# A two-layer decoder on one core: the end of layer 1's cross attention, the routing of its last four tiles, and the shared expert's place, re-ordered

## The chip, the cores and the metric

The kernel runs on one core of a Trainium2 chip. Its time is in device microseconds (us), as the median of several runs; lower is better. PE is the TensorE matmul engine (PEld its weight load), DVE is VectorE, ACT is ScalarE, POOL is GpSimd and SP is SyncE, which issues most transfers. A "send" below is one indirect DMA that POOL issues.

## The reference, cut to what matters

3200 tokens (32 batches of 100) of width 256 go through two decoder layers; each has self attention, cross attention to 361 context rows and a mixture of experts, each on a normalized copy of x and added to x. The change touches the last two blocks of layer 1:

```python
# cross attention: 16 heads of 64, softmax over 361 context rows
attn = softmax(q @ k.T * scale);  x = x + (attn @ v) @ Wo + bo
# experts: 64 in 8 groups, the best 4 groups, then the best 8 experts; 256 places an expert
scores = sigmoid(xn @ gate.T);  topk_idx, topk_w = ...      # routing
out    = sum over a token's experts of  w * w2(silu(xe w1) * (xe w3))
shared = silu(xn @ sg.T) * (xn @ su.T) @ sd.T                # every token
x = x + out + shared
```

## The kernel before, in words

Tokens lie in 25 tiles of 128 rows (`f`), batches are 100 rows (`b`), so a tile is complete when its last batch is.

**Cross attention (`l1_xattn`, L702).** The order of PE is written out by hand. Each batch has 13 steps `s` (L837 on): `scores` (L748; a matmul of 361 columns, DVE's maximum, ACT's exp, DVE's scaling), and three steps later `turn` (L761; three PE transposes, evacuated by ACT to `eT`). At step 3 of batch b the whole of batch b-1 is multiplied with its values (`values`, L769: 48 instructions, evacuated by DVE to `zT`). `between` (L802) puts further work into the steps: the next batch's values (`vals1`), queries (`queries`, `absorbed`, in alternate batches), and `out` (L785), the output projection of a finished tile in two parts, after which DVE adds it to `x` and takes the norm's statistics. `out` stands at steps 1 and 2 of the batch two after the tile's last one; in the last batch also at steps 11 and 12.

**Routing (`route`, L1516).** When the last tile of a group in `ROUTED` (L47: seven groups of three, then two groups of two) is out, a generator is appended to `self.routes`. Each `tick` (L1677) advances each generator by one piece: DVE normalizes the rows, PE turns them and multiplies them with the gate, ACT takes a sigmoid, DVE finds groups and experts, PE counts places (`pp`: operands `tmp`,`before` and `acc`,`ones`), DVE computes `slot`, and then one send per tick: 8 sends a tile (`x_d<-xr,slot`, L1628), each held by `depend` until the last recorded work of its tick. There is one tick a step up to batch 28 and two a step from batch 29 on (L858). The last group (tiles 23 and 24) is advanced by hand in `last_tile` (L820) and in `l1_ffn` (L1698). `list1` (L1639) then makes `listi`, the list of experts in use. `norm_stats` has ACT's Sqrt, the gate ACT's Sigmoid, the softmax ACT's Exp, the experts ACT's Silu: each change between them is one ACT_TABLE_LOAD.

**Shared expert (`shared1`, L1754).** A generator: `hidden(f, i)` is half of the hidden columns of four tiles (8 matmuls of 512 columns on PE, Silu on ACT, a product on DVE), `down(f)` is one tile's second projection (4 matmuls of 256 columns) and DVE's addition to `x`. Before, two `hidden` lie behind the last turns of the cross attention, four `down` around the last tile's norm, then 5 `hidden` and 9 `down` in `l1_ffn` until `FIRST1` = 25 (L59) is used up, and the rest beside the experts' units, about 1 us a unit.

**Units (`units`, L1795).** 24 whole units (256 rows) and 8 half ones. For each, SP issues the expert's weights (`we`, 384 KB, after reading `listi`), and its rows (`xe<-x_d`, up to 321 KB, 8 buffers); the rows wait for `flag` (L1726), which POOL sets when all sends have landed. PE turns the rows (`expert_turn`), multiplies (`expert_hidden`, `expert_add`), DVE weights the result, and POOL adds it to memory by an indirect DMA for each 128 rows (`sum<-ye,xe`, L1897), each behind the landing of the unit two before it. SP issues nine units' weights first, then five units' rows, then a pair a unit. At the end `flag_u` (L1846) releases the loading of the sums, the last additions and the output.

Of the kernel before, what the change touches and what calls it, by code (L numbers as in the profile page):

```python
# [9 lines left out]
F32 = mybir.dt.float32  # L10
# [6 lines left out]
P = 128  # L17
NB = 32
# [25 lines left out]

HALVES = {0: 6, 6: 6, 12: 6, 18: 7}
EDGES = {0: 6, 6: 6, 12: 6, 18: 3, 21: 2, 23: 2}
ROUTED = {**{f: 3 for f in range(0, 21, 3)}, 21: 2, 23: 2}  # L47
FRONT0 = {**{f: 4 for f in range(0, 20, 4)}, 20: 5}
FRONT1 = {0: 4, **{f: 3 for f in range(4, NF, 3)}}
RG = 3  # L50
# [5 lines left out]
WHOLE, HALF = 24, 8  # L56
UNITS = WHOLE + HALF

FIRST1 = 25.0  # L59

BLOCKS0 = 29

# [6 lines left out]
def tile_of(b):  # L69

    f = tiles_before(b + 1)
    return f - 1 if f > tiles_before(b) else None
# [12 lines left out]
class Kernel:  # L85
# [597 lines left out]
    def turn_wk1(self):  # L683

        wk = self.w1x[1]
        for c in range(0, 8, 4):
# [2 lines left out]
                self.nc.tensor.transpose(pt[:, j, :], wk[:, c + j, :], self.ident)  # L689
            self.evac(wk[:, c : c + 4, :], pt, self.ahead_of)  # L690

    def vals1(self, b, half, c):

        if c == 0:
            self.v1[b, half] = self.kv.tile([KC, NKC, 512], F32, tag="v", name="v", bufs=AHEAD)
        t = self.v1[b, half, c] = self.v1[b, half]
        pm = self.bank_p()[:KC, :]
        wv = self.w1x[2]
        self.mm(pm, [(self.ctx1[b][:, c * KC : (c + 1) * KC], wv[:, half * 512 : (half + 1) * 512])])
        return self.evac(t[:, c, :], pm, self.ahead_of)  # L700

    def l1_xattn(self):  # L702
        nc, tc, a = self.nc, self.tc, self.a
        self.route_begin()
        with ExitStack() as st:
# [14 lines left out]
            self.routes = []  # L720
            self.z_begin(pool, 8)
            self.ahead_of = 1

            def queries(b0, u):

# [59 lines left out]
            def out(f, part):  # L785
# [10 lines left out]
                for f0, n in ROUTED.items():  # L796
                    if f0 + n == f + 1 < NF:
                        self.routes.append([self.route(f0, n), None])

            VALS = {4: (0, 0), 5: (0, 1), 6: (0, 2), 7: (1, 0), 9: (1, 1), 10: (1, 2)}  # L800

            def between(b, s):  # L802

                if s in VALS and b + 1 < NB and (b + 1, *VALS[s]) not in self.v1:
                    self.vals1(b + 1, *VALS[s])
                if b % 2 == 0 and b + 2 < NB and s in (8, 11, 12):
                    queries(b + 2, (8, 11, 12).index(s))
                if b % 2 and b + 1 < NB and s == 0:
                    queries(b + 1, 3)
                f = tile_of(b - 2) if b > 1 else None  # L810
                if s in (1, 2) and f is not None:
                    out(f, s - 1)
                if b == NB - 1 and s > 10:
                    out(tile_of(b - 1), s - 11)
                if s == 11 and 0 < b < 5:
                    f = 16 + 2 * b
                    n = min(2, NF - f)
                    self.norm_turn(f, n, self.norm_rows(f, n, bias=self.xbo1), self.bank_p())

            def last_tile():  # L820
                f, shared = NF - 1, self.shared
                for part in range(2):
                    out(f, part)
                    if part == 0:
                        next(shared)
                        next(shared)
                while self.routes:
                    self.tick(self.after)
                r = self.last_route = self.route(NF - 2, 2)
                next(r)  # L830
                next(shared)
                next(shared)

                for _ in range(10):
                    next(r)

            with tc.manual_schedule(engines={mybir.EngineType.PE}):  # L837
                for u in range(4):
                    queries(0, u)
                for p in range(2):  # L840
                    absorbed(0, p, 2)
                for b in range(NB):
                    if b + 2 < NB and b + 2 not in self.ctx1:
                        self.load1(b + 2)
                    for s in range(NS):
                        n = NS * b + s
                        if s < 4:
                            scores(n)
                        if 2 < s < NS - 1:
                            scores(n + 1)  # L850
                        if s == 3 and b > 0:
                            values(b - 1)
                        if s in (3, 8) and b % 2 and b + 1 < NB:
                            absorbed(b + 1, s // 8)
                        between(b, s)
                        if n > 2:
                            turn(n - 3)
                        for _ in range(1 + (b > NB - 4)):  # L858
                            self.tick(self.after)
                n = NS * NB  # L860
                self.shared = self.shared1(first)
                turn(n - 3)
                next(self.shared)
                turn(n - 2)
                turn(n - 1)
                next(self.shared)
                values(NB - 1)
                last_tile()


# [645 lines left out]
    def route(self, f, G):  # L1516
# [7 lines left out]
        if G == RG:  # L1524
            xr = rp.tile([P, RG, XROW], F32, tag="xr", name="xr", bufs=2)
        else:
            xr = self.lnp.tile([P, 2, XROW], F32, tag="xn", name="xr2")
        nc.gpsimd.tensor_copy(xr.bitcast(I32)[:, :, D], self.tok[:, f : f + G])
        for j in range(G):
            self.norm_row(f + j, xr[:, j, :D], nc.vector)  # L1530
# [223 lines left out]
    def shared1(self, first):  # L1754

        nc, x = self.nc, self.x
        wg, wu, wd = self.w1s
        hT = {0: first[:, : 8 * P].rearrange("p (i n) -> p i n", i=2)}

        def hidden(f, i):  # L1760

            n = min(4, NF - f) * P
            if f and i == 0:
                o = f // 4 % 2 * 8 * P
                hT[f] = self.wbs[:, o : o + 8 * P].rearrange("p (i n) -> p i n", i=2)
            pg, pu = self.bank_s()[:, :n], self.bank_t()[:, :n]
            for p, ws in ((pg, wg), (pu, wu)):
                self.mm(p, [(ws[:, k, i * P : (i + 1) * P], self.xn_at(k, f, n // P)) for k in range(NK)])
            g = self.wbs[:, (16 + 4 * i) * P : (20 + 4 * i) * P] if f else first[:, 8 * P : 12 * P]
            nc.scalar.activation(g[:, :n], pg, AF.Silu)  # L1770
            nc.vector.tensor_tensor(hT[f][:, i, :n], pu, g[:, :n], ALU.mult)
            return 3.5

        def down(f):
            pd = self.bank_m()[:, :D]
            h, at = hT[f // 4 * 4], slice(f % 4 * P, (f % 4 + 1) * P)
            self.mm(pd, [(h[:, i, at], wd[:, i, :]) for i in range(2)])
            nc.vector.tensor_tensor(x[:, f, :], pd, x[:, f, :], ALU.add)
            return 0.9

        for i in range(2):
            yield hidden(0, i)
        for f in range(4):
            yield down(f)
        for f in range(4, NF + 4, 4):
            for i in range(2):
                if f < NF:
                    yield hidden(f, i)
                for j in range(2):
                    if f > 4 and f - 4 + 2 * i + j < NF:  # L1790
                        yield down(f - 4 + 2 * i + j)


# [1 line left out]
    def units(self, pool, units, beside=None):  # L1795
# [5 lines left out]
        def weights(i):  # L1801
            we[i] = pool.tile([P, 768], F32, tag="we", name="we", bufs=12)
            u = units[i][0]
            e = nc.sync.value_load(self.listi[0:1, E1 + u : E1 + u + 1], min_val=0, max_val=E1 - 1)
            nc.sync.dma_start(we[i], self.a["wexp"][bass.ds(e, 1)].rearrange("o p n -> p (o n)"))
# [13 lines left out]

        with tc.manual_schedule(engines={mybir.EngineType.PE}):  # L1820
            room = 0.0
            for i in range(9):
                weights(i)
            for i in range(5):
                rows(i)
            for i in range(n_all + 2):
                if i + 5 < n_all:
                    rows(i + 5)
                if i + 9 < n_all:
                    weights(i + 9)  # L1830
                if i < n_all:
                    self.expert_turn(pool, i, len(units[i][1]), xes, xTs)
                if 0 <= i - 1 < n_all:
                    self.expert_hidden(pool, i - 1, len(units[i - 1][1]), we[i - 1], xTs, hTs)

                if beside and i > 2:
                    room = room + 1.0 if i < n_all else 100.0
                    while room > 0:
                        took = next(beside, None)
                        if took is None:  # L1840
                            break
                        room -= took
                if 0 <= i - 2:
                    self.expert_add(pool, i - 2, units[i - 2], we.pop(i - 2), xes, hTs, added, beside)
        flag = pool.tile([1, 1], F32, tag="flag", name="flag_u", bufs=2)
        flag = nc.gpsimd.memset(flag, 0.0)  # L1846
        self.depend(flag, added[0] + added[1], "the units' sums")
# [175 lines left out]
```

## Time and profile before

| what | value |
|---|---|
| median of 3 runs | 3042.85 us (3042.25 to 3046.59) |
| the profiled execution | 3043.06 us, of which the span is 3041.3 us |
| mean granted TensorE clock | 0.978 |
| PE busy | 2905.4 us, 96% of the span |
| DVE, ACT, POOL busy | 1786.2, 1410.3, 910.8 us |
| first turn of a unit's rows | 2877.73 us from the span's start |
| `flag_u` set | 3008.23 us |

Read it so: a line of a timeline has the start, the time taken, the engine, the line, the operation, its tiles (out<-in), the shape and the count of merged instructions, and in brackets how long the engine had sat idle before and what ended that ("issue": nothing that the profile shows). The windows have each engine's busy time in a stretch, the granted clock (1.00 is full), the share of the 16 DMA engines and GB/s. PE carries out each fp32 matmul of the program as two entries, so 48 instructions of `values` are `x96`.

### The profile page before, as it was taken

How to read it: one execution, taken by the hardware profiler on the slowest of the kernel's cores; microseconds unless marked ns; L12 is line 12 of the kernel's file. 1: busy time of each engine (PE TensorE's matmuls, PEld its weight loads, DVE VectorE, ACT ScalarE, POOL GpSimd, SP SyncE). 2: the span in 40 equal slices, each digit the busy share in tenths (PEclk: the TensorE clock that was granted, in tenths of full speed). 3: DMA queues.
4: the chain of work that ended last, by engine and by line, in shares of the span. 5: the costliest groups of instructions: out<-in, count | busy, mean ns of one | idle time of the engine just before them, and what ended most of it. 6: DMA issues, size and time to landing. Idle time of an engine off the chain costs nothing.

```text
span 3041.3 us, 66443 instructions
## 1 busy us (share of the span) xinstructions
PE 2905.4 (96%) x26074; PEld 2210.0 (73%) x26074; DVE 1786.2 (59%) x5048; ACT 1410.3 (46%) x4257; POOL 910.8 (30%) x1038
## 2 busy tenths in 40 slices
PE   8999999999999999999998999999999999998893
PEld 6777777677777757888885667777777777775582
DVE  6666656577777732222225778676676766765353
ACT  5554555566666621222223224556566565665120
POOL 3221222366656543000005530011311302132364
PEclk9999999999999999999999999999999999998997
DMA  8860000000000032555562100000000000000386
GB/s 315 287 242 1 1 1 1 14 17 16 15 15 15 5 116 98 192 188 186 184 232 89 38 2 10 9 30 29 25 14 9 14 9 13 10 12 4 101 207 189
DMA packets 127924, 224.75 MB, mean 74 GB/s; under 512 B 39373, under 2 KB 106245, under 8 KB 120816
## 3 DMA queue, kind: packets, MB, share of 16 engines
q1 hardware_dynamic: 97680, 126.30, 13.0%
q0 software_dynamic: 26640, 90.80, 9.0%
q8 instruction: 210, 3.44, 0.5%
q10 hardware_dynamic: 3280, 3.28, 0.3%
q14 instruction: 114, 0.93, 0.1%
HBM read 152.75 MB, written 112.56 MB: 87 GB/s over the span
## 4 chain that ended last, share of the span: by engine, by line
PE 57%; DVE 3%; DMA 2%; issue 2%; ACT 0%; another core or an unknown queue 0%; POOL 0%; POOLq 0%; SPq 0%; DVEq 0%; ACTq 0%
PE ps_t L141 35%; PE ps_t L778 5%; PE ps_t L766 5%; PE ps_t L1328 4%; PE ps_t L790 3%; PE ps_s L141 2%; DMA sum<-ye,xe 1%; PE ps_m L141 1%; PE ps_t L993 1%; PE ps_t L1334 1%; DMA wA<-sum 1%; DVE s L983 1%; PE ps_t L216 1%; PE ps_t L1272 0%; DVE x_sb L1241 0%
## 5 line engine op out<-in xcount | busy, mean ns | idle before, releaser
L1628 POOL DMA_INDIRECT x_d<-xr,slot x200 | 195.2, 976 | 686.9 <-DVE m L754 396.7
L141 PE MATMUL ps_t<-xnT,wA 128*128 128x200 f32 (+1 forms) x1600 | 326.8, 348 | 1.8 <-DMA wA<-in_wq 1.2
L141 PE MATMUL ps_t<-cT,q 128*128 128x361 f32 x832 | 321.1, 475 | 1.5 <-DVE q L136 1.5
L757 ACT ACTIVATE wBx<-ps_t,m 128x361 f32<-128x361 f32 x416 | 235.0, 566 | 163.2 <-DVE m L754 156.0
L141 PEld LDWEIGHTS ps_t<-xnT,wA 128*128 128x128 f32 x1600 | 270.3, 191 | 31.9 <-issue 14.6
L767 ACT COPY eT<-ps_t 124x384 f32<-124x384 f32 (+1 forms) x416 | 193.3, 474 | 207.9 <-PE ps_t L766 176.7
L141 PE MATMUL ps_t<-xT,w 128*128 128x256 f32 x1276 | 283.2, 381 | 0.7 <-ACT xT L135 0.7
L141 PEld LDWEIGHTS ps_t<-xT,w 128*128 128x128 f32 x1276 | 240.0, 190 | 41.7 <-issue 9.3
L520 DVE TENSOR_REDUCE m<-ps_t 100x1 f32<-100x361 f32 x512 | 239.5, 524 | 48.1 <-PE ps_t L141 47.8
L766 PEld LDWEIGHTS ps_t<-ident,wBx 128*124 128x124 f32 x1248 | 158.1, 141 | 133.1 <-issue 88.4
L754 DVE TENSOR_REDUCE m<-ps_t 128x1 f32<-128x361 f32 x416 | 218.5, 527 | 56.2 <-PE ps_t L141 45.5
L343 POOL TENSOR_TENSOR e<-e,rz 100x400 f32<-100x400 f32 x128 | 109.2, 854 | 407.9 <-DVE rz L342 398.5
L542 ACT ACTIVATE e<-ps_t 121x300 f32<-121x300 f32 x512 | 173.9, 426 | 119.4 <-PE ps_t L141 119.3
L766 PE MATMUL ps_t<-ident,wBx 128*124 128x128 f32 x1248 | 206.0, 277 | 1.8 <-DVE sums L758 1.2
L339 ACT ACTIVATE e<-s,m 100x100 f32<-100x100 f32 x512 | 186.1, 365 | 21.3 <-DVE m L333 20.7
L141 PE MATMUL ps_t<-wA,cT 128*124 128x512 f32 x384 | 194.8, 595 | 1.2 <-PE ps_t L141 1.2
L1309 DVE TENSOR_TENSOR h<-ps_t,g 128x256 f32<-128x256 f32 x145 | 61.1, 424 | 199.5 <-ACT g L1308 199.5
L759 DVE TENSOR_SCALAR wBx<-wBx,sums 128x361 f32<-128x361 f32 x416 | 171.7, 413 | 10.1
L778 PEld LDWEIGHTS ps_t<-eT,v 124*64 124x64 f32 x3072 | 138.0, 139 | 34.8 <-issue 31.0
L758 DVE RECIPROCAL sums<-sums 128x1 f32<-128x1 f32 x416 | 67.1, 161 | 162.3 <-ACT wBx L757 156.0
L778 PE MATMUL ps_t<-eT,v 124*64 124x100 f32 x3072 | 148.3, 254 | 14.1 <-issue 13.8
L141 PEld LDWEIGHTS ps_t<-q,k 32*121 32x121 f32 x3072 | 128.0, 182 | 35.9 <-issue 11.2
(316 smaller groups left out, 5708.8 us busy)
## 6 DMA issues: line engine op xcount, KB each, us to landing
x_d<-fill SPq DMA_DIRECT2D x16, 1284.0 KB
we<-in_wexp SPq DMA_DIRECT2D x32, 384.0 KB
cT<-in_ctxT SPq DMA_DIRECT2D x64, 186.0 KB
xe_d<-zero SPq DMA_DIRECT2D x8, 1024.0 KB
xe<-x_d SPq DMA_DIRECT2D x24, 321.0 KB
xe<-xe_d SPq DMA_DIRECT2D x29, 256.0 KB
y_d<-y SPq DMA_DIRECT2D x29, 256.0 KB
sum<-fill SPq DMA_DIRECT2D x10, 640.0 KB
```

What stands on the lines that cost most here:

```text
L141: self.nc.tensor.matmul(out, lhsT=l, rhs=r, start=(i == 0), stop=(i == n - 1))
L339: nc.scalar.activation(t[:, i, :], s[:, i, :], AF.Exp, bias=m[:, i : i + 1], accum_out=rz[:, i : i + 1])
L520: got = nc.vector.tensor_reduce(m[:, j, o : o + 1], ps[r], AX.X, ALU.max, negate=True)
L542: nc.scalar.activation(t[:, r], ps[r].rearrange("p (c t) -> p c t", c=NKC), AF.Exp)
L754: self.after = nc.vector.tensor_reduce(m, ps, AX.X, ALU.max, negate=True)
L757: nc.scalar.activation(t, ps, AF.Exp, bias=m, accum_out=z)
L759: nc.vector.tensor_scalar(t, t, z, None, ALU.mult)
L766: nc.tensor.transpose(pt[:, c, :], es[n % 5][:, c * KC : (c + 1) * KC], self.ident)
L767: self.after = nc.scalar.copy(eT[:, :, i * P : i * P + w], pt[:, :, :w])
L778: nc.tensor.matmul(pz[64 * j : 64 * j + 64, i, :], lhsT=v[:, c, h * 64 : (h + 1) * 64], rhs=eT[:, c, o : o + T], start=(c == 0), stop=(c = ...
L1328: nc.tensor.matmul(py[s], lhsT=h[:, c, s * P : (s + 1) * P], rhs=w[:, o + c * D : o + (c + 1) * D], start=(c == 0), stop=False,)
L1628: got = nc.gpsimd.indirect_dma_start(out=self.x1_d[:, :], out_offset=bass.IndirectOffsetOnAxis(ap=slot[:, j, k : k + 1], axis=0), in_=xr[: ...
```

## The change

It does six things. `out` moves to steps 5 and 7 of the batch directly after the tile's last one, that is two steps behind that batch's `values`. The last four tiles are routed one by one. There is one tick a step in all batches, and one behind each of the last three turns, and the routes that are left are run out behind the last `values`, ahead of the last tile's `out`. The shared expert's first four tiles and second four tiles are hidden at steps 4, 8 and 11 of the last batch and behind the third last turn (the second four in a `v` buffer), and all eight `down` stand in the last tile's norm and gate. `FIRST1` is 18. SP issues four units' weights, five units' rows, and then the other five weights.

```diff
-ROUTED = {**{f: 3 for f in range(0, 21, 3)}, 21: 2, 23: 2}
+ROUTED = {**{f: 3 for f in range(0, 21, 3)}, **{f: 1 for f in range(21, NF)}}
-FIRST1 = 25.0
+FIRST1 = 18.0
+            self.shared = self.shared1(first)
...
+            OUTS, BESIDE = (5, 7), (4, 8, 11)
...
-                f = tile_of(b - 2) if b > 1 else None
-                if s in (1, 2) and f is not None:
-                    out(f, s - 1)
-                if b == NB - 1 and s > 10:
-                    out(tile_of(b - 1), s - 11)
+                f = tile_of(b - 1) if b else None
+                if s in OUTS and f is not None:
+                    out(f, OUTS.index(s))
+                if b == NB - 1 and s in BESIDE:
+                    next(self.shared)
...
                 for part in range(2):
                     out(f, part)
-                    if part == 0:
-                        next(shared)
-                        next(shared)
-                while self.routes:
-                    self.tick(self.after)
-                r = self.last_route = self.route(NF - 2, 2)
+                r = self.last_route = self.route(f, 1)
+                next(r)
+                for _ in range(4):
+                    next(shared)
                 next(r)
                 next(shared)
-                next(shared)
-                for _ in range(10):
+                next(r)
+                for _ in range(3):
+                    next(shared)
+                for _ in range(8):
                     next(r)
...
-                        for _ in range(1 + (b > NB - 4)):
-                            self.tick(self.after)
+                        self.tick(self.after)
                 n = NS * NB
-                self.shared = self.shared1(first)
-                turn(n - 3)
-                next(self.shared)
-                turn(n - 2)
-                turn(n - 1)
-                next(self.shared)
+                for i in range(n - 3, n):
+                    turn(i)
+                    self.tick(self.after)
+                    if i == n - 3:
+                        next(self.shared)
+                        self.tick(self.after)
                 values(NB - 1)
+                while self.routes:
+                    self.tick(self.after)
                 last_tile()
...
-        for i in range(2):
-            yield hidden(0, i)
-        for f in range(4):
+        for f in (0, 4):
+            for i in range(2):
+                yield hidden(f, i)
+        for f in range(8):
             yield down(f)
-        for f in range(4, NF + 4, 4):
+        for f in range(8, NF + 4, 4):
...
-            for i in range(9):
+            for i in range(4):
                 weights(i)
             for i in range(5):
                 rows(i)
+            for i in range(4, 9):
+                weights(i)
```

More of the change, by code (lines that the diff above doesn't have):

```diff
@@ L690, in turn_wk1, with v_tile @@
             self.evac(wk[:, c : c + 4, :], pt, self.ahead_of)
+    def v_tile(self):
+        return self.kv.tile([P, NKC, 512], F32, tag="v", name="v", bufs=AHEAD)
     def vals1(self, b, half, c):
         if c == 0:
-            self.v1[b, half] = self.kv.tile([KC, NKC, 512], F32, tag="v", name="v", bufs=AHEAD)
+            self.v1[b, half] = self.v_tile()[:KC]
         t = self.v1[b, half, c] = self.v1[b, half]
@@ L1526, in route @@
         else:
-            xr = self.lnp.tile([P, 2, XROW], F32, tag="xn", name="xr2")
+            xr = self.lnp.tile([P, 2, XROW], F32, tag="xn", name="xr2")[:, :G]
         nc.gpsimd.tensor_copy(xr.bitcast(I32)[:, :, D], self.tok[:, f : f + G])
@@ L1757, in shared1 @@
         wg, wu, wd = self.w1s
-        hT = {0: first[:, : 8 * P].rearrange("p (i n) -> p i n", i=2)}
+        bufs = {0: first[:, : 12 * P]}
+        hT = {}
         def hidden(f, i):
             n = min(4, NF - f) * P
-            if f and i == 0:
+            if f == 4 and i == 0:
+                bufs[f] = self.v_tile().rearrange("p c n -> p (c n)")
+            if f in bufs:
+                h, g = bufs[f][:, : 8 * P], bufs[f][:, 8 * P :]
+            else:
                 o = f // 4 % 2 * 8 * P
-                hT[f] = self.wbs[:, o : o + 8 * P].rearrange("p (i n) -> p i n", i=2)
+                h, g = self.wbs[:, o : o + 8 * P], self.wbs[:, (16 + 4 * i) * P : (20 + 4 * i) * P]
+            hT[f] = h.rearrange("p (i n) -> p i n", i=2)
             pg, pu = self.bank_s()[:, :n], self.bank_t()[:, :n]
@@ L1768, in hidden @@
                 self.mm(p, [(ws[:, k, i * P : (i + 1) * P], self.xn_at(k, f, n // P)) for k in range(NK)])
-            g = self.wbs[:, (16 + 4 * i) * P : (20 + 4 * i) * P] if f else first[:, 8 * P : 12 * P]
             nc.scalar.activation(g[:, :n], pg, AF.Silu)
@@ L1789, in shared1 @@
                 for j in range(2):
-                    if f > 4 and f - 4 + 2 * i + j < NF:
+                    if f > 8 and f - 4 + 2 * i + j < NF:
                         yield down(f - 4 + 2 * i + j)
@@ L1834, in units @@
                     self.expert_hidden(pool, i - 1, len(units[i - 1][1]), we[i - 1], xTs, hTs)
-                if beside and i > 2:
-                    room = room + 1.0 if i < n_all else 100.0
+                if beside and 2 < i < n_all:
+                    room += 1.0
                     while room > 0:
@@ L1844, in units @@
                     self.expert_add(pool, i - 2, units[i - 2], we.pop(i - 2), xes, hTs, added, beside)
+            for _ in beside or ():
+                pass
         flag = pool.tile([1, 1], F32, tag="flag", name="flag_u", bufs=2)
```

## Prediction

> **What bounds the kernel now.** I read the windows of 50 us over the end first (us; busy us and counts of PE, PEld, DVE, ACT, POOL; granted clock; DMA share; GB/s):
>
> ```profile
> 2650.00:2700.00 50.00, 50.00 (x335) 36.70 (x334) 37.39 (x134) 34.67 (x85) 12.75 (x13) 1.00 0.05 12
> 2700.00:2750.00 50.00, 43.33 (x338) 31.44 (x337) 27.53 (x95) 20.66 (x58) 23.34 (x24) 0.86 0.03 8
> 2750.00:2800.00 50.00, 42.23 (x260) 30.13 (x261) 32.53 (x121) 30.39 (x76) 3.01 (x4) 0.90 0.01 3
> 2800.00:2850.00 50.00, 41.87 (x217) 25.72 (x216) 18.24 (x74) 10.84 (x16) 15.51 (x17) 0.90 0.02 4
> 2850.00:2900.00 50.00, 44.92 (x171) 30.37 (x172) 17.51 (x48) 9.26 (x18) 22.45 (x21) 0.97 0.64 177
> 2900.00:2950.00 50.00, 49.77 (x241) 40.55 (x240) 27.82 (x71) 12.95 (x28) 36.90 (x24) 1.00 0.95 228
> 2950.00:3000.00 50.00, 38.29 (x224) 31.94 (x222) 23.00 (x70) 10.90 (x29) 35.55 (x23) 1.00 0.70 150
> ```
>
> Up to 2700 PE is busy without a gap: there only less PE work would help. From 2700 to 2870 it has gaps, and the clock falls behind them; from 2870 DMA and POOL are busy too. PE's timeline shows the gaps (start, us, line, shape, count, idle before):
>
> ```profile
> 2703.78 4.34 PE L778 MATMUL ps_t<-eT,v 124*64 124x100 f32 x96
> ...
> 2738.40 0.90 PE L778 MATMUL ps_t<-eT,v 124*64 124x100 f32 x14
> ...
> 2744.59 5.36 PE L778 MATMUL ps_t<-eT,v 124*64 124x100 f32 x77 [0.97 <-issue]
> ...
> 2772.39 1.14 PE L216 MATMUL ps_t<-ident,xr 128*128 128x128 f32 x4 [2.72 <-DVE xr L194]
> ...
> 2790.35 0.77 PE L141 MATMUL ps_t<-tmp,before 128*128 128x128 f32 x2 [5.05 <-DVE tmp L1591]
> ...
> 2809.24 3.17 PE L778 MATMUL ps_t<-eT,v 124*64 124x100 f32 x61
> ```
>
> One `values` takes 4.27 us (2703.78 to 2708.05), but 11.5 from 2738.40 and 12.0 from 2809.24, with gaps of about 1 us that nothing explains ("issue"). POOL's timeline names what runs beside both: sends at their shortest distance, 1.28 us, 13 of them up to 2741.52 and 8 up to 2817.46. `values` is PE's densest stretch of instructions; all I say is that it crawls beside such rows of sends. The other two gaps are routes whose pieces PE reaches too soon.
>
> Then the chain to the units, in POOL's and SP's timelines:
>
> ```profile
> 2846.13 0.97 POOL L1628 DMA_INDIRECT x_d<-xr,slot  x1 [27.70 <-DVE slot L1623]
> ...
> 2865.29 0.97 POOL L1628 DMA_INDIRECT x_d<-xr,slot  x1 [0.30 <-issue]
> 2869.38 0.09 POOL L1726 MEMSET flag<- 1x1 f32 x1 [3.11 <-remote]
> ```
> ```profile
> 2853.85 18.76 SPq L1805 DMA_DIRECT2D we<-in_wexp  x9
> 2873.47 6.16 SPq L1813 DMA_DIRECT2D xe<-x_d  x6
> ```
>
> 16 sends take 20.1 us and land 3.1 us later; SP is still at its nine weights (2.1 us each) and issues the first rows 4.1 us after the flag. PE turns them at 2877.73.
>
> **The change, by stages.** A stage runs from one start of `values` to the next. PE's work in it is a count from the program's order times this trace's rows: a turn 0.33, a score 0.61, a value matmul of 512 columns 0.86, a `values` 4.27, an `out` 3.46, an `absorbed` half 1.55, a query 1.35, a `hidden` 3.44, a `down` 0.87 us.
>
> | stage (starts) | took | PE work before | PE work after | my estimate |
> |---|---|---|---|---|
> | A 2645.52 | 28.5 | 28.2 | 29.5 | 29.8 |
> | B 2673.98 | 29.8 | 29.0 | 27.7 | 28.5 |
> | C 2703.78 | 34.6 | 28.2 | 28.6 | 31.1 |
> | D 2738.40 | 37.4 | 25.5 | 25.7 | 32.2 |
> | E 2775.84 | 33.4 | 24.6 | 31.3 | 35.8 |
> | F 2809.24, to the last `out`'s end | 18.4 | 9.5 | 7.9 | 8.8 |
> | G 2827.64, to `slot` | 18.2 | | | 19.6 |
> | H 2845.85, to the first turn | 31.9 | | | 20.0 |
> | sum | 232.2 | | | 205.8 |
>
> *A, B:* each `out` and route stands nine steps earlier; the sum of their work stays (29.5 + 27.7 against 28.2 + 29.0).
>
> *C, D:* one tick a step instead of two spreads the sends over steps of 1.8 us, so the stalls of 2721 to 2730 and 2738 to 2749 go. What is late next: a single tile's turn stands one step behind its `out`. The same wait in the trace (`out` done 2769.2, xr ready 2772.4) is 3.2 us, of which PE has 1.3 to 2.8 us of work to hide, and a cold clock follows; I leave 2.5 us in C and 4.5 in D.
>
> *E:* two more `hidden` (6.9 us) and tile 23's route, less the 5.05 us gap and its cold clock (2.3). ACT is queued with seven table loads of 1.28 us (2770.10 is such a load), seven exps of 0.75, eight eT copies of 0.48 and four Silus of 0.6: 20.5 us against 31.3 on PE. I leave 2 us for exps behind a table load. The Trainium skill's page "ScalarE: Activation LUTs", section "What ACT_TABLE_LOAD costs", puts a switch at 2.66 us, a drain included; the row has 1.28 us with the next ACTIVATE at once behind it (2771.39). By the page ACT would have 30 us here, still under PE.
>
> *F:* `values` undisturbed (tile 22's eight sends are over by then, paced by the steps), `out` in one piece, no `down` between; 0.8 us for evacuations.
>
> *G:* both PE orders have some 9.5 us of other work between the gate's matmul and `pp`, so a single tile's shorter DVE operations buy little: 17.6 us. But tile 23's eight sends run back to back through its first half, and DVE crawled beside such sends (idle 5.24 us up to 2807.51); I add 2.
>
> *H:* eight sends instead of 16: 10.2 us less. Four weights ahead of the rows instead of nine: SP has `listi` 4.8 us behind `slot`, crawls until the sends end, and can issue the first rows at 14.8 us (the flag is up at 13.4); rows took 3.8 us to land. PE's own work up to there (five `hidden`, six `down`, the list) ends at 18.4. So 18.6, and 1.4 for ACT and DVE being late again (ACT idle 12.58 us up to 2865.89). If the flag were late, the five weights behind the waiting rows would wait with them; their first use is four units (12 us) away.
>
> *Before A:* the same move has a price there. A group of three now has its first sends at steps 10, 11, 12, 0, 1 and 2 around an odd batch's end, where steps take 0.94 us and less: six sends back to back, running into `values`. Before, six sends met `values` twice (from 2424.89 and from 2546.29; it took 9.3 and 7.5 us, 8.2 lost); other groups missed it. Now all six groups meet it. The bounds of one meeting: 0 (a `values` at 2309.41 just behind six sends took 4.4) and 5.0. I take 2.5, as the last two of six sends overlap: 15 - 9 (8.2 and a cold clock) = **+6**. The same 2 to 2.5 is in D and E (tiles 18 to 20 and 21).
>
> The skill's page "Runtime: NRT & Kernel Launch", section "Instruction fetch mechanics", says that instruction fetch is mostly hidden in long unrolled kernels; if so, these stalls are not fetch and need not follow the sends' pace. With the 14.9 us that D's and F's `values` lost kept, and my 10.5 of charges dropped, the sum would be 4 us more.
>
> *Units:* from the first turn to `flag_u` 130.5 us. POOL's 56 additions at 1.85 us make 103.6 of them; the rest are waits for PE, for landings and for rows. 17.3 us of shared work are left beside them instead of 21.6, and the first addition's successor no longer waits for a `hidden`; but five weights (1.97 MB; 6.4 us at the 305 GB/s of 2875 to 2880) come later, into a stage with a DMA share of 0.95. Between -4.3 and +6.4 I take -1.5. *The end:* 33.1 us, unchanged.
>
> **Sum:** 205.8 - 232.2 + 6 - 1.5 = -21.9; 3043.06 - 21.9 = **3021 us** (the profiled execution is 0.2 above the median).
>
> **Rivals.** (1) *The units give it back:* DMA is the bound from 2900 on, the late weights cost 6.4 instead of gaining 1.5: 3021 + 8 = **3029**. For it: shares of 0.95 to 1.1 in windows of 5 us up to 2960. Against it: PE never waited for rows up to 2961. (2) *Nothing crawls:* the meetings cost nothing (-15 - 4.5), and G and H lose 1.5: **3000 to 3003**. For it: stretches of five sends left no gap in PE. (3) *Slower:* the eight meetings (six groups, and `values` of batches 29 and 30) cost what the worst rows show, 7.2 to 7.7 us instead of 2.5: +40, **3061**. Place: L778's successor in every fourth batch. It decides from 5.2 us a meeting on, where the gain is used up. Against it: those rows had longer stretches, and the two shorter meetings lost 5.0 and 3.2. (4) *About 5 us a meeting:* **3041**, no change.
>
> **Chances.** Forecast 0.48 (3010 to 3030), (1) 0.17 (3030 to 3037), (2) 0.20 (up to 3010), (4) 0.07, (3) 0.08. Range 3001 to 3037: it leaves out (3), (4) and the lower part of (2), under 0.2. A difference of 0.2%, 6 us, is about what this measurement can tell from none. Faster by more (below 3036.8): 0.85; within: 0.07; slower: 0.08.
>
> **What would show it.** Right: no `values` over 5 us from batch 28's on except beside six sends; the windows from 2700 at PE 48 or more; `flag` some 13 us behind the last `slot`; the first rows within 2 us of it; the first turn near 2857; `flag_u` some 129 us later. Wrong: `values` of 8 us or more in every fourth batch (rival 3), a `flag_u` over 134 us behind the first turn (rival 1), or a last `slot` over 25 us behind the last `out`.

## The result, and the profile after

The changed kernel took 3051.7 us (median of 13 runs, 3047.08 to 3055.57) where the kernel before took 3042.25 (13 runs): 1.0027 times as long, 95% interval 1.0016 to 1.0038. It is slower, by 8.2 us by this ratio and 9.5 by the medians; the forecast was 3021. The profiled execution took 3049.65 us, with a span of 3047.8.

The windows of 50 us over the end, as shown of before (busy us and counts of PE, PEld, DVE, ACT, POOL; clock; DMA share; GB/s):

```profile
2700.00:2750.00 50.00, 48.37 (x368) 36.03 (x365) 36.58 (x141) 27.35 (x74) 11.71 (x12) 1.00 0.04 10
2750.00:2800.00 50.00, 40.12 (x277) 27.50 (x277) 30.53 (x131) 33.59 (x81) 19.54 (x20) 0.97 0.02 5
2800.00:2850.00 50.00, 47.01 (x305) 33.70 (x306) 25.76 (x100) 24.07 (x46) 13.09 (x16) 0.93 0.02 5
2850.00:2900.00 50.00, 46.07 (x176) 29.54 (x175) 22.86 (x86) 10.70 (x18) 16.60 (x17) 1.00 0.46 137
2900.00:2950.00 50.00, 50.00 (x250) 41.51 (x248) 27.80 (x70) 14.07 (x29) 33.76 (x23) 1.00 0.94 226
```

The gaps of the end have shrunk, except from 2750 to 2800. But everything here is some 20 us late already. PE's timeline shows why. First `values` of batch 13 in the kernel before, which met no send, then the same `values` in the changed kernel:

```profile
2253.66 4.34 PE L778 MATMUL ps_t<-eT,v 124*64 124x100 f32 x96
```
```profile
2261.70 1.94 PE L782 MATMUL ps_t<-eT,v 124*64 124x100 f32 x40
2264.11 0.33 PE L782 MATMUL ps_t<-eT,v 124*64 124x100 f32 x2 [0.48 <-issue]
2264.85 0.25 PE L782 MATMUL ps_t<-eT,v 124*64 124x100 f32 x1 [0.40 <-issue]
2265.56 0.39 PE L782 MATMUL ps_t<-eT,v 124*64 124x100 f32 x3 [0.47 <-issue]
2266.97 3.72 PE L782 MATMUL ps_t<-eT,v 124*64 124x100 f32 x50 [1.02 <-issue]
```

And POOL's timeline of the same stretch:

```profile
2258.47 0.99 POOL L1633 DMA_INDIRECT x_d<-xr,slot  x1 [67.21 <-ACT eT L771]
2259.76 0.97 POOL L1633 DMA_INDIRECT x_d<-xr,slot  x1 [0.30 <-issue]
2261.04 0.97 POOL L1633 DMA_INDIRECT x_d<-xr,slot  x1 [0.30 <-issue]
2262.31 0.98 POOL L1633 DMA_INDIRECT x_d<-xr,slot  x1 [0.30 <-issue]
2263.60 0.98 POOL L1633 DMA_INDIRECT x_d<-xr,slot  x1 [0.30 <-issue]
2264.88 0.98 POOL L1633 DMA_INDIRECT x_d<-xr,slot  x1 [0.30 <-issue]
```

A `values` of 4.34 us takes 8.99: PE runs 40 entries at full speed, then only six in 3.33 us, until 1.1 us after the sixth send is over (2265.86). The next 50 entries take 3.72 us instead of 2.26 at full speed: the granted clock is 0.50 from 2267.83 to 2271.24. All six groups of three have this now: 8.73, 8.63, 8.99, 9.25, 9.37 and 9.24 us. From the first send of each row PE got 54 to 56 weight loads before its first gap; a row of six in which it needs only 43 (before, up to 2308.45) left none.

By the prediction's stages. The two columns on the right are the same two programs run on another chip, of which more below:

| stretch | before | forecast | after | before, chip 3 | after, chip 3 |
|---|---|---|---|---|---|
| start to the first `values` | 1871.7 | 1871.7 | 1869.4 | 1863.8 | 1859.6 |
| first `values` to A | 773.8 | 779.8 | 797.3 | 764.4 | 766.9 |
| A | 28.5 | 29.8 | 31.7 | 28.5 | 31.6 |
| B | 29.8 | 28.5 | 27.8 | 29.8 | 27.8 |
| C | 34.6 | 31.1 | 34.3 | 28.5 | 34.1 |
| D | 37.4 | 32.2 | 35.3 | 30.2 | 33.1 |
| E | 33.4 | 35.8 | 38.7 | 33.4 | 32.2 |
| F, G, H: last `values` to the units' first turn | 68.5 | 48.4 | 50.7 | 54.0 | 46.3 |
| units, to `flag_u` | 130.5 | 129.0 | 130.3 | 128.7 | 129.8 |
| end | 33.1 | 33.1 | 32.4 | 33.1 | 32.3 |
| span | 3041.3 | 3019 | 3047.8 | 2994.3 | 2993.7 |

### The profile page after: what moved, and what is told of

Read it like the earlier page. It is cut to its first block, busy times and chain, and to the rows that moved or that the text cites. A ratio compares the mean times of both kernels' runs of the same rounds, so it can differ in the third digit from the quotient of the medians.

```text
span 3047.8 us, 66590 instructions
## 1 busy us (share of the span) xinstructions
PE 2913.0 (96%) x26082; PEld 2215.3 (73%) x26082; DVE 1790.6 (59%) x5111; ACT 1417.9 (47%) x4270; POOL 914.0 (30%) x1040
## 5 line engine op out<-in xcount | busy, mean ns | idle before, releaser
L782 PE MATMUL ps_t<-eT,v 124*64 124x100 f32 x3072 | 160.5, 262 | 20.7 <-issue 20.7
L782 PEld LDWEIGHTS ps_t<-eT,v 124*64 124x64 f32 x3072 | 148.2, 145 | 42.0 <-issue 30.3
L1313 ACT ACTIVATE g<-ps_t 128x256 f32<-128x256 f32 x145 | 55.6, 383 | 200.4 <-PE ps_t L141 200.4
```

What stands on the lines that cost most here:

```text
L782: nc.tensor.matmul(pz[64 * j : 64 * j + 64, i, :], lhsT=v[:, c, h * 64 : (h + 1) * 64], rhs=eT[:, c, o : o + T], start=(c == 0), stop=(c = ...
```

## The experiments

**Theory.** Beside a row of sends 1.28 us apart PE is given some 55 weight loads and hardly more until the row ends; only `values` (96 loads in 4.3 us) is dense enough to feel it. The moved `out` shifts the sends' phase so that all six groups meet a `values`. **Rivals.** The new place of `out` itself costs the time and the sends are bystanders; or the bytes of the sends do it; or other parts of the change cost it.

**The first runs, on chip 3, met neither.** There the kernel before took 2993.51 us, and nothing was stretched.

`hold_six`, so that the sends pause ahead of `values`:

```diff
-                        self.tick(self.after)
+                        if s > 2 or b % 2 or b > 27:
+                            self.tick(self.after)
```

> The changed kernel, but no tick at steps 0, 1 and 2 of the even batches up to 26, so that the sends of a group of three pause there and the other pieces of its route come up to three steps later. Theory (starved PE): beside a row of sends 1.28 us apart PE gets some 55 weight loads and then hardly any until the row ends, so a `values` of 96 loads in a row of six is stretched from 4.3 to 8.6 - 9.4 us, by gaps of 3.3 us and half speed behind them. Then no `values` before batch 28 is over 4.6 us here, and the time falls by six times 4.9, to about 3022 us (3017 to 3027). Rival (the place of `out`): the new place of `out` costs the time, by its waits, and the sends are only bystanders: 3052 us, with the same long `values`.

1.0006 times before (0.9997 to 1.0014), all `values` 4.34 us.

`out_alone`, the kernel before with `out` at steps 5 and 7 of the next batch:

```diff
-                f = tile_of(b - 2) if b > 1 else None
-                if s in (1, 2) and f is not None:
-                    out(f, s - 1)
-                if b == NB - 1 and s > 10:
-                    out(tile_of(b - 1), s - 11)
+                f = tile_of(b - 1) if b else None
+                if s in (5, 7) and f is not None:
+                    out(f, (5, 7).index(s))
```

> The kernel before, with only `out` moved to steps 5 and 7 of the batch behind the tile's last. Theory (starved PE): all six groups of three now have six sends in a row at the end of an odd batch, so six `values` of 8.6 to 9.4 us (+29), the two of before (9.3 and 7.5, with their half speed about 9) are gone, `out` in its new place costs 0.6 a group (+4), and the end is within 5 us of before: 3042 + 24 = 3066 us (3058 to 3072). If the loss of the whole change comes from its other parts (single tiles, the shared expert, the order of SP): 3042 us or less, with `values` of 4.3.

1.0008 (1.0000 to 1.0017): rows of six meet `values` six times, and it takes 4.34 us.

`narrow_sends`:

```diff
-                    out=self.x1_d[:, :],
+                    out=self.x1n_d[:, :] if f < 18 else self.x1_d[:, :],
...
-                    in_=xr[:, j, :], in_offset=None,
+                    in_=xr[:, j, :16] if f < 18 else xr[:, j, :], in_offset=None,
```

> The changed kernel, but the sends of tiles 0 to 17 carry the first 16 of 321 words of each row, to a place of their own; so 18 tiles' rows never reach the experts (left out), and only the time up to batch 27 is to be read. Theory (POOL's issue of the send holds up the supply): the row of six is still 1.28 us apart and the six `values` still take 8.6 to 9.4 us. Rival (the bytes that the sends move hold up the supply): at a twentieth of the bytes they take 4.3 to 5 us.

4.34 us in all, but so were those of full sends on this chip; it told nothing.

`out_back`, the changed kernel with the removed lines of `out_alone`'s diff in place of the new ones:

> The changed kernel with `out` back at steps 1 and 2 of the batch two behind the tile's last (in the last batch at 11 and 12 too); single tiles, single ticks, the shared expert's place and the order of SP stay. Theory (starved PE): the six meetings are gone (-29), two of before are back (+8 to +9), and the last tiles are routed later (0 to +10): 3031 to 3042 us. Rival (the other parts cost the time): about 3050 us.

0.9984 (0.9975 to 0.9993), on a chip where there were no meetings to lose: so there the new place of `out` costs about 7 us against the old (1.0008 below against 0.9984). By the traces of chip 3 that is nearly all at the end: C to E take 91.8 us with `out` back and 99.4 in the changed kernel, and the way from the first `values` to A is only 0.8 shorter.

**Is it the chip?** (The chip of the measurement isn't recorded.) On chip 3 again, both kernels ran unchanged beside `hold_six`.

> The changed kernel as it is, because in the runs so far the kernel before took 2993.5 us where it took 3042 before, and a row of six sends left `values` at 4.34 us. Theory (the crawl belongs to the conditions of the run, not to the program alone): where the kernel before takes about 2993 us no `values` is over 4.6 us here either, and this takes about what the kernel with held ticks took there, 2994 us (2990 to 2999), no slower than before. Where the kernel before takes about 3042 us the six `values` are 8.6 to 9.4 us again, and this takes 3052. Rival (the held ticks and not the conditions removed the crawl): long `values` and 1.0027 times the kernel before in both.

> The kernel before as it is, for its trace under the same conditions. Where it takes about 2993 us: all `values` 4.3 to 4.5 us, also the two that took 11.5 and 12.0 beside rows of 13 and 8 sends, so the stalls that the change was to remove (about 15 us at the end, 9 at two groups) are not there to be removed. Rival: `values` of 11 to 12 us there as well.

> The changed kernel with no tick at steps 0 to 2 of the even batches up to 26, once more beside the changed kernel itself. Where the kernel before takes about 3042 us: 29 us below the changed kernel, if rows of sends stretch `values`. Where it takes about 2993 us: within 2 us of the changed kernel.

After: 2996.35 against 2994.74 us, 1.0008 (0.9999 to 1.0017). `hold_six`: 1.0001 (0.9990 to 1.0013). The same meeting as above, PE's line and POOL's around it, in the changed kernel on chip 3:

```profile
2241.58 4.34 PE L782 MATMUL ps_t<-eT,v 124*64 124x100 f32 x96
```
```profile
2239.65 0.97 POOL L1633 DMA_INDIRECT x_d<-xr,slot  x1 [0.30 <-issue]
2240.92 0.97 POOL L1633 DMA_INDIRECT x_d<-xr,slot  x1 [0.30 <-ACT wBx L761]
2242.20 0.97 POOL L1633 DMA_INDIRECT x_d<-xr,slot  x1 [0.30 <-issue]
```

The same sends, as close, beside the same `values`, without a gap. In the kernel before, too, the `values` of 11.56 and 12.05 us take 4.34 here:

```profile
2714.96 4.34 PE L778 MATMUL ps_t<-eT,v 124*64 124x100 f32 x96
...
2778.47 4.34 PE L778 MATMUL ps_t<-eT,v 124*64 124x100 f32 x96
```

The stretching depends on the chip, or on the conditions on it, as well as on the program.

`late_turn`, and the waits on PE that it was meant for (the changed kernel's timeline on chip 3):

```profile
2707.14 0.44 PE L216 MATMUL ps_t<-ident,xr 128*128 128x128 f32 x2 [1.63 <-DVE xr L194]
2715.56 0.88 PE L141 MATMUL ps_t<-cT,q 128*128 128x361 f32 x2 [1.42 <-ACT wBx L761]
2718.34 0.52 PE L770 MATMUL ps_t<-ident,wBx 128*124 128x128 f32 x3 [0.86 <-DVE tmp L1587]
2739.71 0.66 PE L216 MATMUL ps_t<-ident,xr 128*128 128x128 f32 x2 [2.88 <-DVE xr L194]
```
```diff
+        if f > 18 and f + G < NF:
+            yield 1
         for j in range(0, G, 2):
...
             self.norm_turn(f + j, n, xr[:, j : j + n, :D], self.bank_t())
```

> The changed kernel with one more empty step between the norm of a single tile (21 to 23) and PE's turn of its rows, which PE waited for 1.63 and 2.88 us with no other work. Theory (a single tile's turn stands too close behind its `out`): those two gaps go, 3 to 5 us less than the changed kernel. Rival (the wait moves on to the gate or to `pp`): within 1.5 us of it.

2992.65 us, 3.7 less than the changed kernel beside it (0.9995 of before, 0.9986 to 1.0004). Part of the wait moved on: PE now waits 2.1 and 1.5 us for later pieces of the route, 1.1 of the 2.88 us are left, and one `values` took 5.73 us.

**The parts by themselves**, on chip 1, where the kernel before took 2992.75 us:

> The changed kernel with the last four tiles routed in two pairs, as before; everything else as changed. Theory (the single tiles are what costs the time at steps behind batch 28: their rows' turn waits for the norm, 1.63 and 2.88 us, with ACT's table loads and DVE's pieces behind it, and save eight sends, 10.2 us, at the end): the first of the two stages before batch 30 is about 5 us shorter, but 16 sends stand behind the last slot again and the first turn of the units' rows comes about 5 us later: within 5 us of the changed kernel, 2996 us where the kernel before takes 2994.7. Rival (single tiles are a loss throughout): 5 us or more below it; rival (a gain throughout): 8 us or more above it.

(`21: 2, 23: 2` again in `ROUTED`, and the last route of two tiles.) 1.0014 (1.0005 to 1.0024). In the traces C is 28.5 us again instead of the 34.1 of chip 3 (C to E 91.7 instead of 99.4), and the way from the last `values` to the units' first turn is 52.6 instead of 46.3: as the theory has it, single tiles lose in C and gain at the end.

> The changed kernel with SP issuing nine units' weights ahead of the first rows, as before. Theory (SP's order matters only where SP is still at the weights when the flag comes; where nothing crawls nine weights take 9.7 us and are over before the flag): within 2 us of the changed kernel where the kernel before takes 2994 us, and 4 to 6 us above it where it takes 3042 (nine weights took 18.8 us there). Rival (the late weights collide with the rows and sums): 3 us or more below it.

(`range(9)` again and no second loop.) 1.0016 (1.0005 to 1.0026), 2.4 us above the changed kernel's ratio on chip 3, where within 2 was expected, but inside the intervals of both; the way from the last `values` to the first turn is 1.7 us longer.

> The changed kernel with `out` of tiles 0 to 17 back at steps 1 and 2 of the batch two behind, where `values` follows it; tiles 18 to 24 as changed. Theory (at its new place `out` is followed by short steps, and PE waits 0.33 us for the first rows of each group and runs at half speed behind that, 0.7 us a group): 4 to 5 us below the changed kernel where nothing crawls, 22 to 27 us below it where rows of sends stretch `values`. Rival (the place of those `out` costs nothing where nothing crawls): within 1.5 us of it.

(The old place for `f < 18`, the new one from 18 on.) 1.0007 (0.9997 to 1.0016): a miss. In the trace the batches from 4 to 23 are as in the kernel before, to 0.02 us, where the changed kernel takes 118.08 us for four batches (8 to 11) instead of 117.33; but at the change-over, in batch 24, it pays 1.2 again, and up to batch 28 only 1.3 us are left.

> Made to beat both kernels: the changed kernel with all `out` back at their old places, one more empty step ahead of a single tile's turn, and no tick at steps 0 to 2 of the even batches up to 26. With only the first of these it took 0.9984 times the kernel before; the second should take away a wait of 2.69 us and its slow clock: 0.997 to 0.998 times the kernel before where nothing crawls, about 0.985 where rows of sends stretch `values`. Rival (the wait moves on to a later piece of the route): 0.9984 again.

(The edits of `out_back`, `late_turn` and `hold_six` together.) 0.9967 (0.9955 to 0.9979).

**On chips that stretch.** The next runs fell on chip 15, where the kernel before took 3046.66 us.

> The changed kernel as it is, a third time, since where a row of sends stretches `values` the test of the six meetings hasn't been run yet. Where the kernel before takes about 3042 us: 1.0027 times it, six `values` of 8.6 to 9.4 us. Where it takes about 2993 us: 1.0008 times it, all `values` 4.34 us.

> The changed kernel with no tick at steps 0 to 2 of the even batches up to 26, beside the changed kernel itself. Where the kernel before takes about 3042 us, theory (six meetings at 4.9 us): 0.993 times the kernel before, 29 us below the changed kernel; rival (the place of `out` itself): 1.0027 again. Where it takes 2993 us: within 2 us of the changed kernel by both.

After: 1.0038 (1.0025 to 1.0050), with six `values` of 9.1 to 10.0 us. With the ticks held: 0.9931 (0.9911 to 0.9950), 35 us less, and no `values` over 4.64 us up to batch 28. In the two traces the six stages with a meeting are 32.1 us shorter, 5.0 to 6.4 each. PE's and POOL's lines of the meeting shown above, now without the last three sends of the row:

```profile
2253.14 4.34 PE L782 MATMUL ps_t<-eT,v 124*64 124x100 f32 x96
```
```profile
2252.47 0.97 POOL L1634 DMA_INDIRECT x_d<-xr,slot  x1 [0.30 <-issue]
2258.80 0.98 POOL L1634 DMA_INDIRECT x_d<-xr,slot  x1 [5.37 <-ACT eT L771]
```

`out` stands where it stood in the changed kernel; only the sends have moved. So the rival with `out` itself falls for these meetings.

> The changed kernel with `out` at its old places, one more step ahead of a single tile's turn, and the held ticks. Where nothing crawls: 0.9967 times the kernel before again. Where rows of sends stretch `values`: 0.983 to 0.988, as the meetings of the kernel before at its batches 20 and 24 (9 us) and at its last three `values` (15 us) are gone too.

0.9902 (0.9886 to 0.9919); less gain than expected. Its last `values` meets eight sends and takes 13.14 us; the way from there to the units' first turn is 61.8 us (48.0 with the same kernel on chip 1), and E is 39.7 (34.6).

`crowded`:

```diff
+                        if b in (5, 6, 9, 10):
+                            for i in range(2):
+                                self.nc.sync.dma_start(self.junk[(2 * n + i) % 8], self.a["ctxT"][:, b, :])
```

> The changed kernel with two more transfers of 186 KB a step, from memory to memory, that nothing reads, in batches 5, 6, 9 and 10 only: beside the first two of the six meetings and not beside the other four. Theory A (a row of sends stretches `values` where transfers of others share what PE's instructions come through): the first two meetings take over 6 us although the other four take 4.34. Theory B (transfers have nothing to do with it): all six 4.34 us where nothing crawls, and all 8.6 to 9.4 where it does.

Void: nothing tied the transfers to their batches. All 104 were issued between 208.0 and 290.8 us, some 1700 us ahead of them, and the DMA share around the meetings is that of the changed kernel (0.15, 0.16 and 0.23 against 0.14, 0.15 and 0.23 in the windows of 20 us from 2000 on).

The last two fell on chip 4, which stretches too (before: 3040.15 us).

> The changed kernel with the sends of tiles 0 to 17 cut to 16 of 321 words a row, to a place of their own (those tiles' rows never reach the experts, so only the time up to batch 27 is to be read). It was run where no row of sends stretched anything; only where the kernel before takes about 3042 us does it tell anything. Theory (POOL's work on a send holds PE's instructions up): the six `values` take 8.6 to 10 us still. Rival (the bytes that the sends move do): 4.3 to 5 us.

The six `values` take 7.5 to 9.0 us. PE's and POOL's lines of one, with a twentieth of the bytes:

```profile
2260.91 2.19 PE L782 MATMUL ps_t<-eT,v 124*64 124x100 f32 x39
2264.22 0.32 PE L782 MATMUL ps_t<-eT,v 124*64 124x100 f32 x2 [1.12 <-issue]
2264.95 0.25 PE L782 MATMUL ps_t<-eT,v 124*64 124x100 f32 x1 [0.41 <-issue]
2265.66 4.26 PE L782 MATMUL ps_t<-eT,v 124*64 124x100 f32 x54 [0.47 <-issue]
```
```profile
2262.35 0.97 POOL L1634 DMA_INDIRECT x1n_d<-xr,slot  x1 [0.30 <-ACT wBx L761]
2263.63 0.97 POOL L1634 DMA_INDIRECT x1n_d<-xr,slot  x1 [0.30 <-issue]
```

A send takes POOL 0.97 us with 16 words a row as with 321. The Trainium skill's page "Perfetto Trace Analysis", section "DMA Instruction — SWDGE (GPSIMD)", says that this time is the writing of descriptors and not the moving of data, with which the row agrees. So the bytes don't decide it. The number of rows and POOL's work on the send stayed as they were; which of these two it comes with, no run parts.

> The kernel before with only `out` moved to steps 5 and 7 of the batch behind. Where the kernel before takes about 2994 us: 1.0008 times it again. Where it takes about 3042 us, theory (the moved `out` alone makes the six meetings): six `values` of 8.6 to 10 us, 1.005 to 1.010 times the kernel before; rival (the single tiles or the other parts are needed for it): within 0.2% of the kernel before.

1.0061 (1.0044 to 1.0078), 19 us slower by the medians, with six `values` of 7.8 to 9.3 us: moving `out` is enough. The same meeting there:

```profile
2260.09 1.94 PE L778 MATMUL ps_t<-eT,v 124*64 124x100 f32 x40
2262.51 0.37 PE L778 MATMUL ps_t<-eT,v 124*64 124x100 f32 x2 [0.49 <-issue]
2263.93 0.41 PE L778 MATMUL ps_t<-eT,v 124*64 124x100 f32 x4 [1.05 <-issue]
2265.36 4.05 PE L778 MATMUL ps_t<-eT,v 124*64 124x100 f32 x50 [1.01 <-issue]
```

## Why the prediction was wrong, point by point

**The step that failed is the price of a meeting.** The prediction named the mechanism, its place (six sends into the `values` of an even batch) and its number (six groups, batches 29 and 30 besides), and then took 2.5 us each, "as the last two of six sends overlap". Between the changed kernel's traces in the measurement and on chip 3 the six stages with a meeting differ by 5.06, 4.89, 4.93, 4.95, 5.03 and 4.90 us: 29.8, where 15 was charged. What counts is not the overlap with `values` but the whole row: some 55 loads are used up in its first 5 us; then, in five of the six rows, PE carries out six entries in 3.3 us; and half speed follows (1.5 us). Both ends of the range, 0 and 5.0, were right for some chip; the value taken between them was right for none.

**Rival (4)** (about 5 us a meeting, 3041 us, chance 0.07) had the size; rival (3) (3061 us) had the side, with 7.2 to 7.7 a meeting, which none of the six groups showed. The span is 28.4 us above the forecast's (3047.8 against 3041.3 - 21.9). Of these 14.8 are the six meetings. D and E are 2.2 and 6.5 us longer than on chip 3, where 2 and 2.5 were charged for a meeting: 4.2 more. These 19.0 alone would have made rival (4)'s "no change" (-21.9 + 19.0); what made the kernel slower is the other 9 us, smaller terms:

- *The place of `out`, costed at nothing.* On chip 3 the changed kernel loses 2.5 us up to A: 0.5 to 0.8 a group from the second on, less 1.1 at the first. At its old place the long `values` covered the wait for the rows' norm; at steps 5 and 7 short steps follow, PE waits 0.32 us for `xr`, and its turns of those rows take 0.92 us where they took 0.66.
- *C.* The wait behind a single tile's `out` was foreseen at 2.5 us. It is 1.63 for `xr`, 1.42 for an exp behind the two table loads of the gate's sigmoid and 0.86 for `tmp`. C took 34.1 us on chip 3, where nothing else disturbs it, 5.5 above PE's 28.6; the other 1.6 aren't traced. The forecast was 3.2 short.
- *D and E without the meetings.* On chip 3 D took 33.1 us, with the wait foreseen (2.88 us), against 25.7 counted and 4.5 added: 2.9 over. E's own work was put 1.1 too high: 32.2 us on chip 3 against 31.3 counted and 2 added.
- *F.* "Undisturbed" was wrong: five of tile 22's sends were still in a row, and `values` took 6.72. F to H are 2.3 us over.

A and B are 1.2 us over, the units and the end 0.6; the time to the first `values` was 2.3 shorter.

**What was right.** F, G and H together are 17.8 us shorter (20.1 foreseen): the flag comes 11.4 us behind the first of the last eight sends, the first rows are issued 2.9 us after it (within 2 foreseen), and PE reaches them as it ends its own work. Part of this size belongs to the chip: on chip 3 the same stretch is only 7.7 us shorter. Units and end are within 1.3 us. Rival (1) (units give it back) did not come: `flag_u` is 130.3 us behind the first turn, below the 134 named for it. ACT's queue in E did not bound it.

**What the prediction could not see.** It priced stalls from one execution as if the program alone made them. The kernel before loses 47 us on the measured chip against chip 3: 7.9 ahead of the first `values`, 9.4 at two groups, 13.5 in C and D, 14.5 from the last `values` to the units, 1.8 after. C, D and F to H, from which the forecast took 28.8 us, hold 28.0 of them, and these aren't there on chip 3. There rival (2)'s "nothing crawls" is true of both kernels, and the change comes out even (1.0008): in the two traces 7.7 us are gained in F to H and 1.2 in E, against 2.5 by `out`'s place, 1.2 in A and B, 5.7 in C, 3.0 in D and 0.3 in the units and the end, 3.8 us more in all from the first `values` on, of which the medians show 1.6.

The page "Runtime: NRT & Kernel Launch", section "Instruction fetch mechanics", on which the prediction weighed a sum without these stalls, says that fetch is mostly hidden. Chips 1 and 3 agree (no gap in any `values`); on chips 4 and 15 PE all but stops for 2.5 to 3.9 us in a row of six with nothing in the trace that it waits for. The traces have transfers of 16 KB in an instruction queue too (queue 8: 210 in each, about 1.0 us each in the median, on chip 3 as where it stretches). They don't go with the gaps: at the meeting from 2631.10 in the measured trace the nearest is over at 2631.54, and from PE's first gap (2633.12) to the end of the stall (2636.38) neither instruction queue has one. Whether the gaps are fetch in another way is not shown.

**Still open:** what a send shares with PE's instructions, and why two of the four numbered chips show it (chip 3 was measured twice, the others once). The try with added transfers missed its place.

## What to carry to other kernels

When a step is moved, look up what its last asynchronous work (here 24 sends, a batch and a half later) will stand beside, and price each meeting by what a row of the same length cost in the trace (5.0 us for the worse of the kernel before's two rows of six) and not by its overlap. A stall that the profile puts down to nothing should be measured on a second chip before a change is built on it. Where two dense streams need not meet, hold one for three steps: it cost nothing where nothing stretched and 35 us less where it did, and with `out` at its old places it made 0.9967 and 0.9902 of the time before.

## What was not expected of the hardware

The same program takes 2993 to 2995 us on chips 1 and 3 and 3040 to 3047 on chips 4 and 15, with sends of the same 0.98 us at the same 1.28 us spacing. On the latter a row of six sends ahead of `values` lets PE have some 55 weight loads (54 to 56 in the measured trace's six rows, 51 to 57 on chips 4 and 15; in the rows of the last stages 44 to 64). Then PE gets a few entries at starts 0.7 or 1.4 us apart, until 0.9 to 1.3 us after the row's last send, with 64 bytes a row as with 1284.
